# Two-layer graph kernel: block 0 of x turned by VectorE, and three reorderings

## Chip, cores and metric

The kernel runs on one core of a Trainium2 chip. The metric is the device time of one execution in microseconds (us), as a median over runs. The engines are named as in the profile: PE is TensorE (PEld its weight loads), DVE is VectorE, ACT is ScalarE, POOL is GpSimd, SP is SyncE, which here only issues DMAs. ACT and POOL issue DMAs too.

## The reference

x is 4096 x 512 (float32), adj is 4096 x 4096 (int32, 0 or 1, about 32 ones in a row). Two layers follow each other, each with a residual and a layer norm.

```python
# layer 0
keep = Ab & (cumsum(Ab, axis=1) <= 64)           # Ab = adj > 0: the first 64 neighbours
cnt = keep.sum(axis=1, keepdims=True)
nb_mean = (keep @ x) / maximum(cnt, 1)
xj = leaky_relu(nb_mean @ W_nb.T + b_nb)
xi = leaky_relu(x @ W_line.T + b_line)
x = layernorm(x + xi + where(cnt > 0, xj, 0))
# layer 1
Wh = x @ W + bW
e = leaky_relu((Wh @ a1 + b1)[:, None] + (Wh @ a2 + b2)[None, :], 0.2)
attention = softmax(where(adj > 0, e, -9e15), axis=1)
x = layernorm(x + attention @ Wh)
```

## The kernel before

The rows of x form 32 blocks of 128. All instructions of an engine run in the order in which the code emits them (`manual_schedule`); engines meet by semaphores only. So the order of the work is written out by hand, and what stands in front of a waiting instruction on its engine is fixed. A hardware DMA of SP or ACT takes one of eight semaphores in turn and waits until the last transfer with that semaphore has landed.

**Opening (layer 0).** The kernel forms y = x @ W_nb.T and the line term x @ W_line.T. A product on PE needs its left operand with the channels on the partitions, so the blocks of x and the weights must be turned. `turn_by_pe` (L310 and L153) does it in four steps: VectorE copies a 128 x 512 tile in another order, PE transposes four 128 x 128 squares of it into PSUM, and ScalarE copies the result to SBUF (L154). Both weight matrices go this way (`turn_w`, one row chunk of 128 at a time, `raw[name][c]`), and so does block 0 of x. The other blocks are turned by `turn_x` in one VectorE instruction (L325), a transpose of 32 x 32 squares; for it `load_turned_x` (L298) brings the block in four DMAs of 64 KB, 512 bytes a piece, so that each square's place is already right. Their landing places are the three tiles of `late`, used in turn. `load_w` (L351) sends the four chunks of a weight matrix to the given queues in turn. `spin` (L357) is a number of transposes of the identity that nobody reads; they fill PE's time while it waits for data.

`linear` (L372) is four matmuls of 128 x 128 by 128 x 512. For block 0 the product with W_nb is split: first its columns 0 to 383, which need only the chunks 0 to 2 of w_nb, then the turning of two chunks of w_line, then the last 128 columns.

`y_terms` splits y into a high part (ScalarE, L420) and a low part (VectorE, L421), both float32r. `line` adds the bias (VectorE, L405), `bend` is the leaky ReLU on ScalarE (L409), `own` stores the term to DRAM by POOL (L416).

**Blocks 2 to 25 (`seven`).** Pairs of blocks are multiplied by seven products instead of eight; `seven(g, ...)` writes out one pair's order, with the end of the pair before in between. PE's products are at L498. In each step g, VectorE adds `tt(bank_w, tg, x_g)` at L582; after it PE may go on adding into `x_g` (the product with `t3` in the next step). That addition waits for two ScalarE copies, L566 (`tg`) and L573 (`t0`).

Into the same steps, at four points `codes[0]` to `codes[3]`, the work on adj is woven. adj comes in chunks of 128 rows by 2048 columns (1 MB, `load_adj`, SP, L164) into two tiles in turn. `edge` (ScalarE, L175) makes flags from a chunk; `scan_sums` and `scan_codes` (VectorE, L193 to L206) count neighbours and make codes; `pack` (ScalarE, L223) turns the codes into bytes, which POOL writes to DRAM (L226). The order in step g, with q the number of the chunk:

```python
first = [lambda: edge(0), lambda: (load_adj(q + 2), edge(q + 1))]
steps = [
    first[g > 2],
    lambda: scan_sums(q),
    (lambda: pack(q - 1)) if g > 2 else first[1],
    lambda: scan_codes(q),
]
```

In g = 3, where q = 1, the flags of the third chunk (`edge(2)`) thus stand at `codes[0]` and the packing of the first chunk at `codes[2]`. In g = 1 the same points carry `fold_w`, sums over the third weight matrix (VectorE, L389).

**After that** come blocks 26 to 31 one by one, the product of the kept flags with y (PE, L750, from 214 to 678 us), layer 1's Wh, and the attention (PE, L1067, from 779 us on).

**Wh of layer 1 (`seven_wh`).** The first two pairs (`PLAIN`) are plain products, L1190; the others, g = 2 to 15, take seven products (PE, L887). In part 0 of a step, PE makes two products, ScalarE copies the first one to `m1` (L906), and VectorE adds `xv[:, 0] = m1 + yr[:, 1]`. For g = 2 that sum stands at L911, ahead of the turning of a later block (`turn_x1`, L833, of a tile that `load_turned` brings by DMA) and of `sums_x1` (L876, L877). For g > 2 it stands at L915, behind them. PE needs the sum for the first product of part 1.

Of the kernel before, what the change touches and what calls it, by code (L numbers as in the profile page):

```python
# [20 lines left out]
P = 128  # L21
SQ = 32
# [10 lines left out]
def two_layer_adj_gnn(  # L33
# [16 lines left out]
    nc = tc.nc  # L50
    N, C = x.shape
# [85 lines left out]
    with ExitStack() as l0:  # L137
# [22 lines left out]
        def load_adj(s):  # L160
            if s < NB * NCH:
                b, h = divmod(s, NCH)
                a = adj_p.tile([P, CH], I32, name="a")
                nc.sync.dma_start(a, adj_blk(b)[:, ts(h, CH)])  # L164
                loaded[s] = a
# [5 lines left out]
        def edge(s):  # L171
            if s < NB * NCH:
                b, h = divmod(s, NCH)
                edge_of[s] = halves_of(adj_p.tile([P, CH], BF16, name="edge"))
                nc.scalar.activation(  # L175
                    edge_of[s], loaded.pop(s).rearrange("p (t q) -> p q t", q=2),
                    AF.Sigmoid, bias=steep[:, 0:1], scale=STEEP,
                    accum_out=cnts[:, h, b : b + 1],
                )
# [39 lines left out]
        def pack(s):  # L219
            if 0 <= s < NB * NCH:  # L220
                b, h = divmod(s, NCH)
                code = adj_p.tile([P, CH // 2], BF16, name="code")
                nc.scalar.copy(  # L223
                    code.bitcast(U8).rearrange("p (t q) -> p q t", q=2), seen_of.pop(s)
                )
                nc.gpsimd.dma_start(code_d[b][:, ts(h, CH // 2)], code)  # L226
# [56 lines left out]
        with ExitStack() as la:  # L283
# [9 lines left out]
            def load_turned_x(i, queue=nc.gpsimd):  # L293

                if i < NB:
                    xrs[i] = late[i % 3].rearrange("p (j c) -> p j c", c=P)
                    for n in range(NC):
                        queue.dma_start(  # L298
                            xrs[i][ts(n, SQ)],
                            x_blk(i)[:, ts(n, P)].rearrange("(j a) c -> a j c", a=SQ),  # L300
                        )

            def load_own_x(i, queue):
                xbs[i] = work.tile([P, C], F32, name="xb", bufs=1)
                queue.dma_start(xbs[i], x_blk(i))

            def turn_by_pe(dst, src):

                t = work.tile([P, C], F32, name="t", bufs=4)
                nc.vector.tensor_copy(  # L310
                    t.rearrange("p (m n b) -> p m n b", m=NC, b=SQ),
                    src.rearrange("p (n m b) -> p m n b", m=NC, b=SQ),
                )
                transpose_to(dst, lambda m: t[:, ts(m, P)], NC)
# [4 lines left out]
            def turn_x(i, t=None):  # L319
                if i < NB:  # L320
                    xts[i] = xt_tile() if t is None else t
                    if i == 0:
                        turn_by_pe(xts[i], xbs[i])
                    else:
                        nc.vector.transpose(  # L325
                            xts[i].rearrange("p m (j a) -> p j m a", a=SQ),
                            xrs.pop(i).rearrange("p j (m b) -> p j m b", b=SQ),
                        )


            def early(name):
# [17 lines left out]
            def load_w(name, src, queues):  # L349
                for c in range(NC):  # L350
                    queues[c % len(queues)].dma_start(raw[name][c], src[ts(c, P), :])  # L351

            def spin(n):

                idle = ps_acc.tile([P, P], F32, name="acc")
                for _ in range(n):
                    nc.tensor.transpose(idle, ident, ident)  # L357

            def turn_w(name, idle=0, parts=range(NC)):

                if name not in w_t:
                    w_t[name] = wp.tile([P, NC, C], F32, name=f"wt_{name}")
                for c in parts:
                    if idle:
                        spin(idle)
                    turn_by_pe(w_t[name][:, :, ts(c, P)], raw[name][c])

            def linear(lhs_t, name, bank=None, part=slice(0, C)):

                pl = ps_acc.tile([P, C], F32, name="acc") if bank is None else bank  # L370
                for k in range(NC):
                    nc.tensor.matmul(  # L372
                        pl[:, part], lhs_t[:, k, :], w_t[name][:, k, part],
                        start=(k == 0 and part.start == 0),
                        stop=(k == NC - 1 and part.stop == C),
                        skip_group_check=part.stop - part.start < C,
                    )
                return pl

            def load_rows(queue):  # L380
# [37 lines left out]
            def y_terms(i, src):  # L418

                nc.scalar.copy(y_hi[i], src)  # L420
                return lambda: nc.vector.tensor_tensor(  # L421
                    y_lo[i], src, y_hi[i].bitcast(F32), ALU.subtract
                )

            load_own_x(0, nc.sync)
            load_w("nb", w_nb, (nc.scalar, nc.sync))
            load_turned_x(1, nc.sync)
            load_w("line", w_line, (nc.scalar, nc.sync))
            nc.sync.dma_start(bias_line, b_line.partition_broadcast(P))
            spin(15)  # L430


            turn_x(0)
            turn_w("nb", 2)

            for i in (2, 3):
                nc.vector.memset(late[i % 3][:, 0:1], 0.0)
                load_turned_x(i)
            pys[0] = linear(xts[0], "nb", part=slice(0, 3 * P))
            turn_w("line", 0, range(0, 2))  # L440
            linear(xts[0], "nb", pys[0], slice(3 * P, C))
            turn_w("line", 0, range(2, 4))
# [60 lines left out]
            turn_pair(1, 0)  # L503
            tt(t1, w12, w11, ALU.subtract)
            tt(t2, w22, t1, ALU.subtract)
            y_low = y_terms(0, pys[0])
            x_low[1] = xt_tile()
            turn_pair(1, 1)
            y_low()
            line(0)  # L510
            bend(0)
            pls[1] = linear(xts.pop(1), "line")
            wide.append(pls[1])
            x_top[0] = xt_tile()
            y_low = y_terms(1, pys[1])
            sums_x(1)
            own(0)
            y_low()
            load_adj(0)
            line(1)  # L520
            bend(1)
# [77 lines left out]
            for g in range(1, EDGE // 2):  # L599
                steps = idle  # L600
                q = done[0]
                if g == 1:
                    steps = [
                        lambda: (load_adj(1), fold_w(0)),
                        lambda: (fold_w(1), fold_w(2)),
                        idle[0],
                        lambda: (fold_w(3), fold_w(NC), fold_end()),
                    ]
                else:
                    first = [lambda: edge(0), lambda: (load_adj(q + 2), edge(q + 1))]  # L610
                    steps = [
                        first[g > 2],
                        lambda: scan_sums(q),
                        (lambda: pack(q - 1)) if g > 2 else first[1],
                        lambda: scan_codes(q),
                    ]
                    done[0] += 1
                seven(g, False, steps)
# [112 lines left out]
        for s in range(NB * NS):  # L731
            i, g = divmod(s, NS)
# [159 lines left out]
    def seven_wh(g, part, extra=lambda: None):  # L892

        p = g - 1
        new, old = g < NS // 2, p >= PLAIN
        yr, xv = yrs[g % 2], xvs[g % 2]
        yr_p, xv_p = yrs[p % 2], xvs[p % 2]
        t1, t2, t3, t4 = wsums  # L900
        m1 = bt[:, g, 2] if new else None
        if part == 0:
            if new:
                product_wh(yr[:, 0], x1ts[2 * g][:, 0:2], w11, start=True)
                product_wh(yr[:, 1], x1ts[2 * g + 1][:, 0:2], t3)
                nc.scalar.copy(m1, yr[:, 0])  # L906
            if old:
                product_wh(yr_p[:, 0], x1ts.pop(2 * p)[:, 2:4], w21)
                product_wh(xv_p[:, 1], sum_x(p, 1), t1)
            if g == PLAIN:  # L910
                nc.vector.tensor_tensor(xv[:, 0], m1, yr[:, 1], ALU.add)  # L911
            turn_x1(2 * g + 3)
            sums_x1(g + 1)
            if new and g > PLAIN:
                nc.vector.tensor_tensor(xv[:, 0], m1, yr[:, 1], ALU.add)  # L915
            if old:
                nc.scalar.copy(bt[:, p, 0:2], yr_p)
            extra()
        else:
            if old:  # L920
                product_wh(xv_p[:, 0], x1ts.pop(2 * p + 1)[:, 2:4], t4)
            if new:
                product_wh(xv[:, 0], sum_x(g, 2), t2)
                product_wh(yr[:, 1], sum_x(g, 4), w22)
            turn_x1(2 * g + 4)
            sums_x2(g + 1)
            if old:
                nc.scalar.copy(bt[:, p, 2:4], xv_p)
                later.append(p)
            if new:  # L930
                nc.scalar.copy(xv[:, 1], xv[:, 0])
            extra()
# [384 lines left out]
```

## Time and profile before

| | us |
|---|---|
| median of 3 runs | 1560.03 (1559.98 to 1561.58) |
| the profiled execution, its own time | 1561.81 |
| the profiled execution, its span | 1559.9 |
| PE busy | 1546.9 |
| VectorE busy | 1261.9 |
| ScalarE busy | 980.1 |

The page describes one profiled execution. Its span runs from the first to the last instruction; the time of that execution is 1.9 us more, and lies 1.8 us above the median of the other runs. A line of a timeline gives the start, the time taken, the engine, the line of the kernel, the operation, what it writes and reads, and in brackets how long the engine had been idle before it and what ended that. A float32 matmul is recorded as two passes, so x8 stands for four matmuls.

### The profile page before, as it was taken

What the parts mean: (1) busy time and instruction counts of PE and PEld (TensorE: products, weight loads), DVE (VectorE), ACT (ScalarE), POOL (GpSimd) and SP (SyncE); (2) the same over time, 40 slices, a digit from 0 to 9 for tenths busy, and PEclk for the clock granted to TensorE, in tenths of its full rate; (3) what the DMA queues carried; (4) which work ended last, traced back from release to release, by engine and by line L of the source; (5) the groups of instructions that cost most, each with busy time, mean ns of one, the idle gap of its engine ahead of it and who ended that gap; (6) DMA issues with size and microseconds to landing.
All of it is one profiled execution on the core that took longest, in us unless ns stands there. A gap on an engine that the chain in (4) does not pass through costs nothing.

```text
span 1559.9 us, 19141 instructions
## 1 busy us (share of the span) xinstructions
PE 1546.9 (99%) x6587; PEld 1242.7 (80%) x6587; DVE 1261.9 (81%) x2339; ACT 980.1 (63%) x1183; POOL 266.4 (17%) x424
## 2 busy tenths in 40 slices
PE   9999999999999999999999999999999999999998
PEld 5444468888888888868888888888888888888887
DVE  6888658999999999469888788887888878888864
ACT  2776558887888878427684576555775556755520
POOL 4554212222122122110001001110011110111101
PEclk9999999999999999999999999999999999999999
DMA  8866469988898988654122122221222211222102
GB/s 236 205 219 203 155 175 256 249 257 259 241 257 242 255 217 239 141 132 114 50 55 67 34 49 69 55 68 38 44 69 56 66 43 39 69 62 61 49 6 54
DMA packets 175425, 201.17 MB, mean 129 GB/s; under 512 B 102032, under 2 KB 135568, under 8 KB 167136
## 3 DMA queue, kind: packets, MB, share of 16 engines
q1 hardware_dynamic: 147472, 130.33, 30.4%
q0 software_dynamic: 26224, 67.64, 16.9%
q10 hardware_dynamic: 1632, 1.98, 0.4%
q8 instruction: 51, 0.84, 0.2%
q14 instruction: 46, 0.38, 0.1%
HBM read 141.03 MB, written 42.08 MB: 117 GB/s over the span
## 4 chain that ended last, share of the span: by engine, by line
PE 95%; DMA 2%; DVE 2%; issue 1%; ACT 0%; ACTq 0%; POOL 0%; POOLq 0%; DVEq 0%
PE acc L1067 35%; PE acc L750 30%; PE pt L1067 14%; PE acc L498 7%; PE acc L887 5%; PE acc L372 3%; DMA a<-in_adj_dram 1%; DMA w<-x_d 1%; PE pt L372 0%; PE pt L153 0%; PE acc L357 0%; DVE edge L389 0%; ACT edge L175 0%; DMA nat<-code_d 0%; DVE y_lo L421 0%
## 5 line engine op out<-in xcount | busy, mean ns | idle before, releaser
L1067 PE MATMUL acc<-bt,s 128*128 128x256 f32 x1504 | 335.7, 379 | 0.0
L750 PE MATMUL acc<-y_hi,kt 128*128 128x512 f32 x824 | 320.5, 389 | 0.0
L750 PE MATMUL acc<-y_lo,kt 128*128 128x512 f32 x824 | 320.5, 389 | 0.0
L1067 PEld LDWEIGHTS acc<-bt,s 128*128 128x128 f32 x1504 | 285.8, 190 | 38.9
L952 ACT ACTIVATE w<-nat,few 128x1024 f32<-128x1024 uint8 x128 | 137.0, 1136 | 237.8 <-DVE a L1027 237.8
L1067 PE MATMUL acc<-bt,a 128*128 128x256 f32 x1056 | 239.0, 379 | 0.0
L1067 PE MATMUL pt<-bt,a 128*128 128x256 f32 x992 | 224.5, 379 | 0.0
L1067 PEld LDWEIGHTS acc<-bt,a 128*128 128x128 f32 x1056 | 200.6, 190 | 27.3
L1067 PEld LDWEIGHTS pt<-bt,a 128*128 128x128 f32 x992 | 188.5, 190 | 25.6
L1027 DVE STREAM_TRANSPOSE a<-w 128x1024 f32<-128x1024 f32 x128 | 153.1, 1225 | 61.8 <-ACT w L1008 51.0
L277 ACT ACTIVATE kt<-ktb,few 128x1024 fp32r<-128x1024 uint8 x124 | 142.7, 1151 | 96.0 <-PE acc L750 76.7
L126 POOL TENSOR_TENSOR rs<-ve,few 128x1 f32<-128x1 f32 x64 | 44.8, 700 | 810.8 <-DVE ve L124 810.6
L750 PEld LDWEIGHTS acc<-y_hi,kt 128*128 128x128 f32 x824 | 154.7, 188 | 32.1
L750 PEld LDWEIGHTS acc<-y_lo,kt 128*128 128x128 f32 x824 | 154.6, 188 | 32.1
L945 ACT ACTIVATE w<-w,st_n 128x1024 f32<-128x1024 f32 x128 | 149.3, 1232 | 16.1 <-DVE m L962 16.1
L1008 ACT ACTIVATE w<-w,nm 128x1024 f32<-128x1024 f32 x128 | 145.5, 1138 | 11.1 <-DVE nm L999 11.1
L962 DVE CUSTOM_DVE_ANT_0 w<-e_n,w 128x1024 f32<-128x1024 f32 x128 | 149.5, 1221 | 1.3
L175 ACT ACTIVATE edge<-a,few 128x2048 bf16<-128x2048 int32 x64 | 136.2, 2128 | 9.5 <-DMA a<-in_adj_dram 5.3
L223 ACT CAST code<-left 128x2048 uint8<-128x2048 bf16 x64 | 121.1, 1892 | 0.0
L206 DVE TENSOR_TENSOR left<-edge,left 128x2048 bf16<-128x2048 bf16 x64 | 78.4, 1225 | 2.2
L298 POOL DMA_DIRECT2D c<-in_x_dram x120 | 66.1, 558 | 68.9 <-DVE xt L325 54.1
L194 DVE TENSOR_TENSOR_SCAN left<-few,ends,left 128x1024 bf16<-128x1024 f32 x32 | 75.2, 2351 | 1.1
(225 smaller groups left out, 2004.9 us busy)
## 6 DMA issues: line engine op xcount, KB each, us to landing
a<-in_adj_dram SPq DMA_DIRECT2D x64, 1024.0 KB, 6.3
code_d<-code POOLq DMA_DIRECT2D x64, 256.0 KB, 4.4
nat<-code_d SPq DMA_DIRECT2D x248, 64.0 KB, 2.2
w<-x_d SPq DMA_DIRECT2D x128, 64.0 KB, 2.1
own<-in_x_dram SPq DMA_DIRECT2D x31, 256.0 KB, 3.4
own<-own_d POOLq DMA_DIRECT2D x31, 256.0 KB, 5.0
x_d<-own POOLq DMA_DIRECT2D x31, 256.0 KB, 5.1
c<-in_x_dram POOLq DMA_DIRECT2D x120, 64.0 KB, 5.0
```

The lines of the kernel that those rows point to most:

```text
L175: nc.scalar.activation(edge_of[s], loaded.pop(s).rearrange("p (t q) -> p q t", q=2), AF.Sigmoid, bias=steep[:, 0:1], scale=STEEP, accum_ou ...
L206: nc.vector.tensor_tensor(left, e, left, ALU.mult)
L223: nc.scalar.copy(code.bitcast(U8).rearrange("p (t q) -> p q t", q=2), seen_of.pop(s))
L277: nc.scalar.activation(kts[s], bytes_.rearrange("p t (i r) -> p t r i", r=2), AF.Sigmoid, bias=steep[:, 1:2], scale=STEEP,)
L498: nc.tensor.matmul(bank, lhs[:, k, :], rhs[:, k, :], start=start and k == 0, stop=k == 1, skip_group_check=True,)
L750: nc.tensor.matmul(accs[i], kt[:, k // 2, k % 2, :], term[j], start=(j == 0 and term is y_hi), stop=(j == NB - 1 and term is y_lo),)
L945: nc.scalar.activation(dst, src, AF.Prelu, bias=bias, scale=scale, alpha=0.2)
L952: nc.scalar.activation(wts[b][:, i, :], nats[b, i // 2].bitcast(U8)[:, i % 2, :], AF.Relu, bias=far, scale=-FAR,)
L962: nc.vector.tensor_tensor_reduce(w_i, e2_n, w_i, 1.0, -3e38, ALU.subtract, ALU.max, m4s[b][:, i : i + 1])
L1008: nc.scalar.activation(w_i, w_i, AF.Exp, bias=nms[b][:, i : i + 1], accum_out=z4s[g][:, r, i : i + 1])
L1027: nc.vector.transpose(a[:, r].rearrange("p s (i a) -> p i s a", a=SQ), wts[2 * g + r][:, :, ts(k, 8 * SQ)].rearrange("p i (s x) -> p i s x ...
L1067: nc.tensor.matmul(banks[g][n], lhs[:, j, :], bt[:, 4 * k + j, rhs, :], start=(k == 0 and j == 0 and n == mate[0]), stop=(k == NP - 1 and ...
```

## The change

1. Block 0 of x is loaded in four DMAs like the others, ahead of everything else on SP, and turned by VectorE. The chunks 0 and 1 of w_nb are loaded by ACT and 2 and 3 by SP, instead of in alternation. On PE, 14 idle transposes stand at the start instead of 15. The chunks 0 to 2 of w_nb are turned, two idle transposes ahead of each, then block 0 on VectorE; the chunk 3 is turned behind the first matmul of block 0's product, without idle transposes.
2. The two y terms of blocks 0 and 1 are emitted together, ahead of the turning of block 3 and of block 0's line term. Before, they stood behind and between these.
3. In g = 3 of `seven`, the packing of the first chunk and the flags of the third change places. (In g = 2 and from g = 4 on, the order stays.)
4. In `seven_wh`, the sum for g = 3 stands ahead of the turning, as for g = 2.

```diff
             def turn_x(i, t=None):
                 if i < NB:
                     xts[i] = xt_tile() if t is None else t
-                    if i == 0:
-                        turn_by_pe(xts[i], xbs[i])
-                    else:
-                        nc.vector.transpose(...)
+                    nc.vector.transpose(
+                        xts[i].rearrange("p m (j a) -> p j m a", a=SQ),
+                        xrs.pop(i).rearrange("p j (m b) -> p j m b", b=SQ),
+                    )
...
-            def linear(lhs_t, name, bank=None, part=slice(0, C)):
+            def linear(lhs_t, name, bank=None, part=slice(0, C), behind_first=lambda: None):
...
+                    if k == 0:
+                        behind_first()
...
-            load_own_x(0, nc.sync)
-            load_w("nb", w_nb, (nc.scalar, nc.sync))
+            load_turned_x(0, nc.sync)
+            load_w("nb", w_nb, (nc.scalar, nc.scalar, nc.sync, nc.sync))
             load_turned_x(1, nc.sync)
             load_w("line", w_line, (nc.scalar, nc.sync))
             nc.sync.dma_start(bias_line, b_line.partition_broadcast(P))
-            spin(15)
-            turn_x(0)
-            turn_w("nb", 2)
+            spin(14)
+            turn_w("nb", 2, range(3))
+            turn_x(0)
             for i in (2, 3):
                 nc.vector.memset(late[i % 3][:, 0:1], 0.0)
                 load_turned_x(i)
-            pys[0] = linear(xts[0], "nb", part=slice(0, 3 * P))
+            pys[0] = linear(
+                xts[0], "nb", part=slice(0, 3 * P), behind_first=lambda: turn_w("nb", 0, range(3, 4))
+            )
...
-            y_low = y_terms(0, pys[0])
+            for i in range(2):
+                y_terms(i, pys[i])()
             x_low[1] = xt_tile()
             turn_pair(1, 1)
-            y_low()
             line(0)
             bend(0)
             pls[1] = linear(xts.pop(1), "line")
             wide.append(pls[1])
             x_top[0] = xt_tile()
-            y_low = y_terms(1, pys[1])
             sums_x(1)
             own(0)
-            y_low()
             load_adj(0)
...
-                    first = [lambda: edge(0), lambda: (load_adj(q + 2), edge(q + 1))]
+                    flags = lambda: (load_adj(q + 2), edge(q + 1))
+                    codes = (lambda: pack(q - 1)) if g > 2 else (lambda: edge(0))
                     steps = [
-                        first[g > 2],
+                        flags if g > 3 else codes,
                         lambda: scan_sums(q),
-                        (lambda: pack(q - 1)) if g > 2 else first[1],
+                        codes if g > 3 else flags,
                         lambda: scan_codes(q),
                     ]
...
-            if g == PLAIN:
+            if g < PLAIN + 2:
                 nc.vector.tensor_tensor(xv[:, 0], m1, yr[:, 1], ALU.add)
             turn_x1(2 * g + 3)
             sums_x1(g + 1)
-            if new and g > PLAIN:
+            if new and g >= PLAIN + 2:
                 nc.vector.tensor_tensor(xv[:, 0], m1, yr[:, 1], ALU.add)
```

More of the change, by code (lines that the diff above doesn't have):

```diff
@@ L321, in turn_x @@
                     xts[i] = xt_tile() if t is None else t
-                    if i == 0:
-                        turn_by_pe(xts[i], xbs[i])
-                    else:
[L325 to L328, printed above, removed]
+                    nc.vector.transpose(
+                        xts[i].rearrange("p m (j a) -> p j m a", a=SQ),
+                        xrs.pop(i).rearrange("p j (m b) -> p j m b", b=SQ),
+                    )
             def early(name):
```

## The prediction

> **What bounds the kernel now.** I read the page first, for the busy shares and the chain that ended last.
>
> ```profile
> PE 1546.9 (99%) x6587; PEld 1242.7 (80%) x6587; DVE 1261.9 (81%) x2339; ACT 980.1 (63%) x1183; POOL 266.4 (17%) x424
> ...
> PE 95%; DMA 2%; DVE 2%; issue 1%; ACT 0%; ACTq 0%; POOL 0%; POOLq 0%; DVEq 0%
> ```
>
> TensorE (PE) is busy 1546.9 of 1559.9 us. The change removes no work from it but four transposes and three of the idle transposes that fill the opening. So it can gain only where PE stands still or does filler. The view of waits, for PE alone, has all standstills but the end:
>
> ```profile
> PE acc L498 <- DVE acc L582: 2.1, 3, 1.2
> PE acc L357 <- POOL ident masks.py:199: 1.4, 1, 1.4
> PE acc L887 <- DVE acc L911: 0.9, 1, 0.9
> PE acc L887 <- DVE acc L915: 0.8, 1, 0.8
> PE acc L498 <- DVE y_lo L421: 0.4, 1, 0.4
> ```
>
> Without the 1.4 us before the first instruction, 4.2 us are to be had. 0.2% of 1560 us, about what a measurement of this kernel can tell from no change, is 3.1 us. PE's timeline places the waits (start, duration, then the idle time before):
>
> ```profile
> 8.97 2.85 PE L372 MATMUL acc<-wt_nb,xt 128*128 128x384 f32 x8
> ...
> 25.16 1.98 PE L498 MATMUL acc<-wt_nb,xt 128*128 128x512 f32 x4 [0.41 <-DVE y_lo L421]
> ...
> 34.33 1.98 PE L498 MATMUL acc<-wt_line,xt 128*128 128x512 f32 x4 [0.28 <-DVE acc L582]
> ...
> 60.94 1.98 PE L498 MATMUL acc<-wt_line,lo 128*128 128x512 f32 x4 [1.23 <-DVE acc L582]
> ```
>
> From 8.97 to 24.6 and from 60.94 to 678 us PE never waits, so a time won or lost at the front stays to the end, if the others keep up. Of L582's three waits the one not shown is 0.59 us at 47.44. A stall costs about 0.16 us more than its idle time: the product before it could have been followed after 59.55 (eight passes of 0.43 from 56.12), not after its modelled end.
>
> **What the Trainium skill says.** "VectorE: DVE Perf Modes", The three transpose paths: VectorE turns only 32x32 blocks, so the rest of the turning must lie in the load. The trace agrees: one STREAM_TRANSPOSE of 128x512 f32, 0.70 us, after four loads of 64 KB. "DMA: Bandwidth & Descriptors", Queues, rings and completion order: SP and ACT have a ring each on the same 16 engines, which serve the rings in turn. The trace agrees: from 3 to 4 us 93 packets of SP's queue and 100 of ACT's. "TensorE: Matmul & The Clock Gate", Part 1: PE starts throttled, speeds up after about 3.4 us of work, and falls back after as long an idle stretch. The trace agrees on the start (0.23 us for one idle transpose at first, 0.11 after 6.4 us); it has no idle gap that long, so the fall is not shown.
>
> **The change, part by part.** Below, nb0 to nb3 and line0 to line3 are the four row chunks of w_nb and w_line; x0 and x1 are the blocks of x.
>
> *Block 0 turned by VectorE (opening).* Removed: a VectorE copy (0.43), four PE transposes, a ScalarE copy (0.59). Added: one STREAM_TRANSPOSE (0.70) and three more DMA issues on SP (0.3 to 0.4 each), as x0 now comes in four pieces. The first products need nb0 to nb2; now nb0, nb1 lie on ACT's queue and nb2, nb3 on SP's behind x0's pieces. DMA is full from 3 us on (share 1.03 to 1.10 in the windows), so order decides. In the packet records a 2048-byte packet takes 84 ns and a 512-byte one 27 to 30, so a 256 KB chunk is 128 x 84 / 16 = 0.67 us of all engines and an x piece 0.24. Now the loads landed at 4.55 (two chunks done, 1.34 of work), 5.8 (four, 2.69) and 7.5 (six and one piece, 4.27): work plus 3.2. After: before nb2 come x0 (0.96), nb0, nb1, line0, line2 (2.69), then itself: 4.32 + 3.2 = 7.5; 6.85 if line2 still stands behind it. I take 7.4. nb2's path is then copy 0.38, transposes 0.44, ScalarE copy 0.59 and three hand-overs of 0.1: first product at 9.1 instead of 8.97. x0 lands earlier, and its transpose ends inside this path. nb3's four transposes, which PE did before 8.97, now stand behind the first product: 0.44 and 0.1 for the hand-over. **Sum: 0.7 us lost; I take 0.6.** Bounds: -0.5 (nb2 at 6.3, small packets going ahead), +1.5 (nb2 at 8.3). Queued behind: nb3 and then x1's pieces and line1, line3 on SP (issues that wait for earlier landings; line1 now for line2's). Total bytes are the same and line1 landed at 10.1 for a need at 12.1, so that is hidden by 2 us. POOL's loads of x2 and x3 start after the two memsets, about 1 us later; x2 is first needed at 24.6, and was turned at 14.1: hidden. VectorE's later work is hidden by its 3.7 us of idle time before 21.36.
>
> *Two y terms sooner.* y_lo of blocks 0 and 1 (0.57, 0.60) leave the stretch from 22.0 to 25.0 and go into VectorE's idle time before 21.36; ScalarE's y_hi of block 1 follows, 6 us sooner (ScalarE idle 7.7 us). PE's wait at 25.16 goes. But the next wait, at 34.33, is for VectorE's L582, and VectorE runs without a gap from 21.36 to 34.27. It gets 1.17 us free, yet line(1) must wait for PE's end of block 1's line product at 24.76; it starts at 24.85 instead of 25.02. So only **0.2 us** of 0.57 is kept, and the waits at 34.33 and 47.44 remain, the former larger. Bounds: 0.1 and 0.3.
>
> *Flags of the third chunk later.* ScalarE's timeline:
>
> ```profile
> 51.65 0.57 ACT L556 COPY acc<-acc 128x512 f32<-128x512 f32 x1 [3.22 <-DVE y_lo L421]
> 55.78 2.15 ACT L175 ACTIVATE edge<-a,few 128x2048 bf16<-128x2048 int32 x1 [3.56 <-DMA a<-in_adj_dram]
> ...
> 59.58 0.58 ACT L573 ACTIVATE t<-acc 128x512 f32<-128x512 f32 x1
> 60.06 1.89 ACT L223 CAST code<-left 128x2048 uint8<-128x2048 bf16 x1
> ```
>
> ScalarE waits 3.56 us for the chunk with four operations queued behind it; L582 waits for the last (L573), PE for L582. Now pack (1.89, its input ready at 50.4) takes that place: 52.2 to 54.1, the four follow to about 56.4, and L582 comes at 56.9, bound by VectorE's own scan, against PE's need at 59.5. The flags start at 56.4, after the landing at 55.8, and end at 58.6, when ScalarE's next copies are due and VectorE is still busy to 60.6. **Gain 1.39 us** (1.23 and 0.16). SP: the fourth chunk's load waits on flags of the second, done at 47.4 as before; the fifth is issued at about 58.7 instead of 58.0. POOL: the code write (0.56) comes 8 us sooner, ahead of four loads of x issued at 55.6. What is late next: the fourth chunk landed at 59.5 and its flags, still first in g = 4, come up at about 62; 256 KB more in a full DMA costs it 0.7. Cover 1.8 us; if it is gone, up to 1.4 comes back.
>
> *One sum of wh sooner (g = 3).*
>
> ```profile
> 699.68 0.71 DVE L833 STREAM_TRANSPOSE a<-w 128x512 f32<-128x512 f32 x1 [0.59 <-DMA w<-x_d]
> 700.43 0.43 DVE L876 TENSOR_TENSOR bt<-a 128x256 f32<-128x256 f32 x1
> 700.89 0.42 DVE L877 TENSOR_TENSOR a<-a 128x256 f32<-128x256 f32 x1
> 701.23 0.42 DVE L915 TENSOR_TENSOR acc<-bt,acc 128x256 f32<-128x256 f32 x1
> ```
>
> The sum's ScalarE input is ready at 698.76. It now goes at 699.1, in the 0.59 us that VectorE waits for a load, so transpose and differences keep their times. PE, that started the product at 701.71, can at 700.8: **0.9 us** (0.5 to 0.93: VectorE is dense to 713, and the sum of g = 5 is then just in time).
>
> **Sum** against the profiled execution (span 1559.9, its own time 1561.8, 1.8 above the median): 0.6 - 0.2 - 1.4 - 0.9 = -1.9 us. I apply the difference to the median 1560.03: **1558.1 us**.
>
> **Rivals.** (A) As summed, 1558.1; 0.50. (B) The opening pays too: the removed copies had held nb0 to nb2 up (nb2 landed at 5.8, its PE transposes started only at 7.67), so if nb2 lands by 6.3 the opening gains 0.6 and with 2.5 the sum is -3.1 or more: 1556.8. Against it: four ACT chunks stand in turn with x0. 0.24. (C) A stall comes back: the fourth chunk's flags hold ScalarE in g = 4, or wh's later sums hold PE: 1559.4. For it: DMA full from 52 to 65 us. 0.20. (D) Slower: PE runs dry in the opening. After two chunks and its fillers it has nothing from about 6.4; if nb2 lands at 9.4, the gains are eaten; from about 10.2 (line1's landing now) the gap is over the skill's 3.4 us, and PE's clock falls back: an estimate of 3.4 us at half speed, 1.7 us. Then 3.3 + 1.7 - 2.5: 1562.5, past 0.2% from nb2 at 10.9. Against it: nb2 waits only for nb0's landing. 0.06.
>
> **How the numbers follow.** B alone is faster by over 0.2%: 0.24. A and C are within: 0.70. D: 0.06. The range runs from just under B's value, 1556.6, to just short of no change, 1559.9; A's own, from its bounds, is 1557.0 to 1559.2.
>
> **What would show it.** Right: the first 128x384 product at about 9.1; no PE wait at 60 us nor on L916 near 701; the one after g = 1 (L581) 0.3 larger; ScalarE's pack at 52 us. Wrong: a PE wait on L581 near 71, a first product after 10, an idle transposes' pace of 0.23 us again after 7 us, or one before 8.5, which is B.

## The result, and the profile after

The kernel after takes 1562.75 us (median of 22 runs, 1560.35 to 1564.61), the kernel before 1560.03 (22 runs, 1559.05 to 1562.14). The ratio is 1.0018, 95% interval [1.0011, 1.0024]: 2.8 us slower, [1.7, 3.7], where 1.9 us faster was forecast; the median lies outside the predicted range, 1556.6 to 1559.9. The profiled execution of after has a span of 1562.8 us and an own time of 1564.61. That is 1.9 us above its median, as before's was 1.8 above its own, but it is also the longest of the 22, so what is read off this profile is after at its worst.

The page of after, busy shares and the chain that ended last:

```profile
PE 1548.9 (99%) x6580; PEld 1243.4 (80%) x6580; DVE 1262.6 (81%) x2339; ACT 981.2 (63%) x1182; POOL 268.4 (17%) x424
...
PE 97%; DVE 1%; DMA 1%; ACT 0%; issue 0%; SPq 0%; POOLq 0%; DVEq 0%; ACTq 0%
```

TensorE has seven instructions fewer (four transposes, three idle ones), and yet 2.0 us more busy time. It worked at a lower pace somewhere. PE's waits (us in total, times, longest):

```profile
PE pt L153 <- DVE t L310: 2.2, 2, 2.0
PE acc L354 <- POOL ident masks.py:199: 1.4, 1, 1.4
PE acc L888 <- DVE acc L912: 0.9, 1, 0.9
PE acc L499 <- DVE acc L581: 0.9, 2, 0.6
PE acc L369 <- ACT wt_nb L154: 0.7, 1, 0.7
PE acc L888 <- DVE acc L916: 0.2, 1, 0.2
PE acc L499 <- ACT acc L596: 0.2, 1, 0.2
```

Against before, the 1.23 us at 61 us, in step g = 3 (L582 then, L581 now), the 0.41 us on y_lo and the 0.76 us on a sum of wh are gone or small. New are 1.96 us at the turning of w_nb (the copy L310) and 0.68 us at the first product (ScalarE's copy of the turned chunk, L154). PE's timeline (start, duration; idle time before, with its releaser):

```profile
7.04 0.38 PE L354 MATMUL acc<-ident 128*128 128x128 f32 x2
9.37 0.78 PE L153 MATMUL pt<-ident,t 128*128 128x128 f32 x4 [1.96 <-DVE t L310]
10.82 1.65 PE L369 MATMUL acc<-wt_nb,xt 128*128 128x384 f32 x2 [0.68 <-ACT wt_nb L154]
12.27 1.06 PE L153 MATMUL pt<-ident,t 128*128 128x128 f32 x4
13.12 3.80 PE L369 MATMUL acc<-wt_nb,xt 128*128 128x384 f32 x6
16.76 1.04 PE L153 MATMUL pt<-ident,t 128*128 128x128 f32 x8
```

The first product starts at 10.82 (before: 8.97), the transposes of line0 and line1 behind it at 16.76 (before: 11.65). So 5.11 us are lost by 17 us. The view of windows, in which the number in front of the DMA share is the granted clock of TensorE, says how:

```profile
9.00:10.00 1.00, 0.63 (x4) 0.42 (x4) 0.97 (x5) 0.00 (x0) 0.00 (x0) 0.86 1.26 210
10.00:16.00 6.00, 5.32 (x12) 3.25 (x12) 3.18 (x8) 1.17 (x2) 5.81 (x10) 0.50 0.83 213
16.00:17.00 1.00, 1.00 (x5) 0.49 (x5) 0.00 (x0) 0.00 (x0) 1.00 (x3) 0.73 0.99 336
```

PE ran at half speed from 9.72 to 16.55 (the ends are from the clock's own records); before, all these windows stood at 1.00. The loss of 5.11 us can be split, with the full-clock run e4 as the yardstick:

- the first product is later by 10.82 - 8.97 = 1.85 us;
- nb3's transposes now lie inside the product: where the clock is full (e4 below) it takes 3.13 us from its start to line0's transposes, before it took 2.68: 0.45 us;
- at half clock the same stretch takes 5.94 us: 5.94 - 3.13 = 2.81 us.

Later parts give back some of it. The shift of equal products, after less before, is +4.88 at the wait at 39.21, +3.51 at the y product at 64.45 and +2.37 at 705.04; it ends at +2.9, the difference of the spans. All these shifts compare one execution with one other. The seven profiles with the old opening (before, e1, e5, e6, e7, e10, e11) start the transposes of line0 between 10.93 and 13.78 us, at 11.70 on average, so before's 11.65 is a fair measure of it.

### The profile page after: what moved, and what is told of

It is laid out like the page before. It is cut to its first block, busy times and chain, and to the rows that moved or that the text cites. A ratio compares the mean times of both kernels' runs of the same rounds, so it can differ in the third digit from the quotient of the medians.

```text
span 1562.8 us, 19137 instructions
## 1 busy us (share of the span) xinstructions
PE 1548.9 (99%) x6580; PEld 1243.4 (80%) x6580; DVE 1262.6 (81%) x2339; ACT 981.2 (63%) x1182; POOL 268.4 (17%) x424
## 3 DMA queue, kind: packets, MB, share of 16 engines
q10 hardware_dynamic: 1632, 1.98, 0.5%
## 4 chain that ended last, share of the span: by engine, by line
PE 97%; DVE 1%; DMA 1%; ACT 0%; issue 0%; SPq 0%; POOLq 0%; DVEq 0%; ACTq 0%
PE acc L1068 35%; PE acc L751 30%; PE pt L1068 14%; PE acc L499 8%; PE acc L888 5%; PE acc L369 3%; PE acc L1191 1%; DMA a<-in_L_gnn_W_nb_dram 1%; PE pt L369 0%; DVE edge L388 0%; PE pt L153 0%; DVE left L194 0%; ACT edge L175 0%; DMA nat<-code_d 0%; ACT L175 0%
```

## Experiments

Theory T: the opening loses the time, through a first product that comes late and a clock that falls in the gap ahead of it; the other three parts pay about what was forecast. Rivals: lateness alone, the clock being a bystander; a later part costs what it should have won; and, once sizes came in, that the forecast gains belonged to one execution. Differences below are the ratio's excess over 1, times 1560 us. Each ratio is taken against the kernel before at the same time on the same chip; the median of before there was 1559.75 to 1561.26 us. So two changed kernels measured at different times are compared through their ratios.

### e1_rest_only and e2_open_only: where the loss lies

e1 is after with the opening of before, e2 is before with the new opening alone. The edit of e1 (e2 is its complement: these lines as in after, all others as in before):

```diff
-            load_turned_x(0, nc.sync)
-            load_w("nb", w_nb, (nc.scalar, nc.scalar, nc.sync, nc.sync))
+            load_own_x(0, nc.sync)
+            load_w("nb", w_nb, (nc.scalar, nc.sync))
...
-            turn_w("nb", 2, range(3))
             turn_x(0)     # i == 0: turn_by_pe again
+            turn_w("nb", 2)
...
```

> The changed kernel with the opening of before (block 0 turned by PE, w_nb in alternation on the two queues); the y terms, the flags and the sum of wh stay changed. Theory (the whole loss lies in the opening): the three reorderings bring 0.2 + 1.4 + 0.6 = 2.2 us, so about 1557.8 us, first 128x384 product at 9.0 us. Rival (a part of the loss lies in the reorderings, through later waits of POOL or SP): 1559 or more.

> The kernel before with the new opening alone. Theory: first product at about 10.8 us and the opening 5.1 us later at its end, of which 2.8 are PE's half clock: about 1565 us, with a wide spread between executions[...]. Rival (the opening is late by its data alone, 2.3 us): 1562.3. Rival (the old stalls at 34, 47 and 61 us swallow a part): 1563.

Measured: e1 ratio 0.9988 [0.9982, 0.9995], 1.9 us faster. e2 1.0022 [1.0014, 1.0029], 3.4 us slower [2.2, 4.5]; its profile shows a gap of 1.85 us, a first product at 10.60 and the clock at half from 8.80 to 15.63. The loss lies in the opening, and the three later parts together gain; that they cost what they should have won is ruled out.

Two expectations missed. The first product of e1, with the old opening, was expected at 9.0 and came at 11.10:

```profile
11.10 2.85 PE L372 MATMUL acc<-wt_nb,xt 128*128 128x384 f32 x8
```

In that execution block 0 was copied at 5.26 (before: 4.38), and the clock's record shows full speed only from 10.0 us (before: 6.5). So the old opening has late executions too.

e2 was expected 5.1 us over before, with a wide spread, and is 3.4. The 5.1 had been read off a profile with the clock at half, and the clock doesn't fall in every execution. For each execution the clock granted over the whole span is on record, to three places. An execution with 0.999 lost less than 2.4 us to a lower clock. In the profiles the end of the kernel alone takes 1.2 to 2.5 us, and a fall of 3.41 us in the opening takes 1.7 more; so with 0.999 there was no fall in the opening. One with 0.997 or less lost over 3.9 us, so there was one; 0.998 leaves it open. In e2 the five executions with 0.999 have a median of 1563.35, 2.1 us above before, and the five with 0.997 or less one of 1566.14, 4.9 above. The same opening thus costs about 2 us where it is only late, and 2.8 more where the clock falls. In after, 11 of 22 executions have 0.997, 10 have 0.998 and one has 0.999.

### e3_fill and e9_half_fill: lateness or clock

e3 fills PE's gaps with idle transposes and moves nothing else; e9 fills half of the first gap.

```diff
-            turn_w("nb", 2, range(3))
+            turn_w("nb", 2, range(2))
+            turn_w("nb", 20, range(2, 3))     # e9: 10 in place of 20
             turn_x(0)
...
+            spin(5)                           # e3 alone
             pys[0] = linear(xts[0], "nb", ...
```

> The changed kernel with 20 idle transposes instead of 2 ahead of the third chunk of w_nb and 5 ahead of the first product, so that PE is not idle while it waits; transfers unchanged. Theory (2.8 us of the loss are the clock): PE clock full from 6 us on, third chunk lands at 8.8 as before, first product at about 10.8, the end of the first part 2.8 us sooner: about 1560.0 us. Rival (the products behind 10.8 are slow because they wait for data): no change, 1562.7.

> The kernel after with 10 idle transposes instead of 2 ahead of the third chunk of w_nb, and none ahead of the first product: by 0.11 us each (20 took 2.35 us) they leave about 1.0 us of the 1.96 us gap, and the 0.68 us gap ahead of the first product stays. If an idle stretch has to fill about 2 us before the clock falls, the clock holds and the time is that of the kernel with the whole gap filled, 1.0 to 1.3 us over before's 1560 less the gains of the other parts: about 1560. If what counts is idle time in the fixed 3.4 us stretch, however it is cut up, 1.0 + 0.68 us of idleness is near what the kernel after had and the clock falls in some or all executions: about 1562.5. If lateness alone made the loss, also 1562.5, with a full clock in the profile.

e3: 0.9999 [0.9991, 1.0008], so 3.0 us better than after (the two intervals lie 0.5 us apart). Its timeline:

```profile
9.33 0.63 PE L153 MATMUL pt<-ident,t 128*128 128x128 f32 x4
9.79 0.71 PE L354 MATMUL acc<-ident 128*128 128x128 f32 x5
10.63 0.91 PE L369 MATMUL acc<-wt_nb,xt 128*128 128x384 f32 x2
11.38 0.60 PE L153 MATMUL pt<-ident,t 128*128 128x128 f32 x4
11.82 2.10 PE L369 MATMUL acc<-wt_nb,xt 128*128 128x384 f32 x6
13.75 1.04 PE L153 MATMUL pt<-ident,t 128*128 128x128 f32 x8
```

The chunk's transposes and the first product come as late as in after (9.33 and 10.63 for 9.37 and 10.82), but six products take 2.10 us instead of 3.80. "Lateness alone" is refuted: work that computes nothing gives 3.0 us back, against 2.81 us read off the timeline. What e3 still lacks to e1 is 1.7 us, against 2.3 of lateness in the split above.

e9: 1.0003 [0.9995, 1.0011], 2.3 us better than after. Its timeline:

```profile
9.41 0.63 PE L153 MATMUL pt<-ident,t 128*128 128x128 f32 x4 [1.10 <-DVE t L310]
10.72 1.37 PE L369 MATMUL acc<-wt_nb,xt 128*128 128x384 f32 x2 [0.68 <-DVE t L310]
11.88 1.06 PE L153 MATMUL pt<-ident,t 128*128 128x128 f32 x4
12.73 2.96 PE L369 MATMUL acc<-wt_nb,xt 128*128 128x384 f32 x6
```

In this execution the clock fell at 11.04 for 3.41 us, half as long as in after, and no single gap was over 1.10 us. So a fall doesn't need one long gap: 1.10 + 0.68 us of idleness within one stretch of 3.41 us (7.63 to 11.04) went ahead of this one. The time lies near the case "the clock holds", the profile shows a fall. The granted clocks agree with both: the profiled execution is the longest of 13, ten have 0.999 (median 1561.0), and the three with 0.998 are the longest (1562.26 to 1563.26). In most executions half the filling was enough.

### e4_nb_act and e8_x_pool: can nb2 come sooner

SP issues nb2 late in after. SP's timeline of after, and its waits up to 20 us:

```profile
0.75 1.82 SPq L298 DMA_DIRECT2D c<-in_x_dram  x4
4.76 0.83 SPq L348 DMA_DIRECT2D a<-in_L_gnn_W_nb_dram  x2
```

```profile
SPq L348 <- DMA a<-in_L_gnn_W_nb_dram: 2.5, 2, 2.2
```

SP has x0's four pieces out by 2.6 and then stands until 4.76, because nb2's issue waits for nb0's landing (4.74). nb2 lands at 8.77, 4.0 us later, as nb0 took from its issue. There are two candidates for the lateness: this wait, and the place behind x0's pieces in SP's queue. e4 gives nb2 to ACT's queue; e8 leaves w_nb alternating and gives x0 to POOL's queue.

```diff
 e4:
-            load_w("nb", w_nb, (nc.scalar, nc.scalar, nc.sync, nc.sync))
+            load_w("nb", w_nb, (nc.scalar, nc.scalar, nc.scalar, nc.sync))
 e8:
-            load_turned_x(0, nc.sync)
-            load_w("nb", w_nb, (nc.scalar, nc.scalar, nc.sync, nc.sync))
+            load_turned_x(0)
+            load_w("nb", w_nb, (nc.scalar, nc.sync))
```

> The changed kernel with the third chunk of w_nb on ACT's queue ahead of w_line, so that it does not wait on SP for the first chunk's landing nor stand behind block 0's pieces. Theory (the place in the queue made it late, and the gap made the clock fall): it lands at about 7.3 as the fifth 256 KB of both queues, PE's gap is 0.6 us, clock full, first product at 9.4: about 1558.7 us. Rival (the pieces of 512 bytes slow every packet beside them, so the chunk is late in any queue): lands after 8.3, 1561 or more.

> The changed kernel with block 0's four pieces on POOL's queue and w_nb in alternation on ACT and SP as before. Theory (the pieces ahead on SP made w_nb late): the first three chunks land by 5.8 us as before or sooner, the pieces at about 6.5 to 7, the first product starts at about 8.0, clock full: 2.5 us less than before on the same chip. Rival (pieces of 512 bytes delay everything beside them in any queue, or POOL's issue is too slow): first product after 9, less than 1.5 us gained.

e4: 0.9989 [0.9983, 0.9996], 1.7 us faster than before. Its timeline:

```profile
7.57 0.60 PE L153 MATMUL pt<-ident,t 128*128 128x128 f32 x4
8.84 0.91 PE L369 MATMUL acc<-wt_nb,xt 128*128 128x384 f32 x2 [0.68 <-ACT wt_nb L154]
9.59 0.60 PE L153 MATMUL pt<-ident,t 128*128 128x128 f32 x4
10.03 2.10 PE L369 MATMUL acc<-wt_nb,xt 128*128 128x384 f32 x6
11.97 1.04 PE L153 MATMUL pt<-ident,t 128*128 128x128 f32 x8
```

nb2 is copied at 6.59 instead of 8.80, the gap ahead of its transposes is gone, the 0.68 us gap alone leaves the clock full, and line0's transposes start at 11.97. So one word in a list of queues turns the change's loss into a gain. It stands level with e1 (1.9), so block 0's turning by VectorE is worth nothing measurable even where its loads come right. e4 and e1 are both a little faster than before and than after; these runs don't tell which is the better.

The packet records tell the two candidates apart. In after, SP's queue moves x0's packets of 512 bytes until 6.63 us, in turn with ACT's of 2048 bytes, and nb2's first packet starts at 7.14. In e4 it is nb3 that stands behind x0 on SP. It is issued at 3.84, 0.9 us sooner than nb2 in after, and yet its first packet starts only at 6.64, when x0's last ones go out. So by these two executions an earlier issue could have brought nb2 forward by 0.5 us at most; the rest goes with its place behind the small packets. 256 KB in packets of 512 bytes held SP's queue until 6.6 us, as long as 768 KB in packets of 2048 did in before (until about 6.5).

e8 missed: 1.0028 [1.0018, 1.0038], 4.4 us slower. nb2 was copied at 6.11, but x0's pieces, issued by POOL from 1.5 to 3.9, landed only by 10.6, and the first product, at 11.42, had waited 3.97 us for block 0's turning, with the clock at half from 12.75 to 16.16. A late load, PE idle, then the clock at half: the path is the same as in after, with another load.

### e5_only_flags, e6_only_sum, e7_only_y: the other parts singly

Each is before with one part of the change:

```diff
 e5 (flags):
-                        first[g > 2],
+                        flags if g > 3 else codes,
...
-                        (lambda: pack(q - 1)) if g > 2 else first[1],
+                        codes if g > 3 else flags,
 e6 (sum):
-            if g == PLAIN:
+            if g < PLAIN + 2:
...
-            if new and g > PLAIN:
+            if new and g >= PLAIN + 2:
 e7 (y):
-            y_low = y_terms(0, pys[0])
+            for i in range(2):
+                y_terms(i, pys[i])()
... (the old places of the y terms are emptied)
```

> The kernel before with the exchange of pack and flags in g = 3 alone. Theory: the PE wait of 1.2 us near 61 us goes and nothing takes its place: 1.4 us less than before on the same chip. Rival (the fourth chunk's flags in g = 4 stall ScalarE in its turn): a PE wait near 71 to 73 us and less than 0.7 us gained.

> The kernel before with the sum of wh for g = 3 ahead of the turning, alone. Theory: the PE wait of 0.8 us at 701.7 goes (0.9 us in starts), and a part comes back at the sum of g = 5, because VectorE's turning waits for a load and is not earlier: a wait of 0.2 to 0.3 us on that sum, 0.6 us net. Rival (as predicted, 0.9 us net): no PE wait on that sum.

> The kernel before with the y terms of blocks 0 and 1 together, alone. Theory: the PE wait at 25 us (0.41) goes, about 0.2 us is kept, the waits at 34 and 47 us stay at 0.3 and 0.6, since VectorE must wait for block 1's line product: 0.2 us less, not to be told from nothing by the times. Rival (VectorE is freed by 1.2 us): the waits at 34 and 47 us go, 1 us or more gained.

Measured: e5 0.9997 [0.9989, 1.0006], 0.5 us faster; e6 0.9994 [0.9986, 1.0002], 0.9; e7 1.0000 [0.9992, 1.0008]. No interval leaves out either the forecast or zero, so the times of single parts settle nothing here; their sum, 1.4, goes with e1's 1.9. In the profiles each part does what was expected of it: in e5 no stall at 61 us and none near 71; in e6 the stall on the sum of g = 3 gone and 0.41 us on the sum of g = 5; in e7 the 0.41 us on y_lo gone, the waits at 33 and 47 us at 0.28 and 0.60. The profiles tell more, for an unexpected reason: in e6 and e7, which leave the flags where they were, the stall of 1.23 us at 61 us is absent.

### e10_y_and_sum and e11_before_again: how firm is the stall at 61 us

e10 is before with the parts of e6 and e7 together; e11 is the kernel before, unedited, in a new execution.

> The kernel before with two of the four parts alone: the y terms sooner and the wh sum sooner; opening and flags as before. If the flags' stall of 1.23 us at 61 us stands in every execution and putting the flags later takes 1.4 us out, then this kernel lacks that gain: 1.9 - 1.4 = 0.5 us below before, 1559.5. If the stall comes and goes with the landing of the third chunk of adj, as the two runs whose profiles lacked it suggest, it lacks little: 1.0 to 1.9 us below before, 1558.1 to 1559.

> The kernel before, unchanged, in another execution: does the stall on the y product at 61 us (1.23 us in its first profile, 1.31 us with the new opening, absent in two others that left the flags in place) stand? If the flags' order alone makes it, 1.2 to 1.3 us again. If the landing of the third chunk of adj makes it, anything from 0 to 1.3 us, and the wait of the third chunk's flags for their load moves with it (3.56 us in the first profile, 2.26 and 1.98 us where the stall was absent).

e10: 0.9997 [0.9988, 1.0005], 0.5 us faster, nearer to the case "the flags lack 1.4" and with an interval that holds both. e11, one execution: 1560.5 us, with a stall of 0.88 us. ScalarE's timeline of e11 has the wait for the third chunk of adj, PE's the stall that follows:

```profile
55.05 2.16 ACT L175 ACTIVATE edge<-a,few 128x2048 bf16<-128x2048 int32 x1 [3.20 <-DMA a<-in_adj_dram]
```

```profile
60.22 1.98 PE L498 MATMUL acc<-wt_line,lo 128*128 128x512 f32 x4 [0.88 <-DVE acc L582]
```

The same of e6, ScalarE's timeline and PE's waits up to 80 us:

```profile
53.85 2.16 ACT L175 ACTIVATE edge<-a,few 128x2048 bf16<-128x2048 int32 x1 [2.26 <-DMA a<-in_adj_dram]
```

```profile
PE acc L500 <- DVE acc L584: 0.9, 2, 0.6
```

In e6 L584 (the L582 of before) is waited for twice, at 34 and 47 us, and not at 61. Over the six profiles that keep the flags' old order:

| kernel | ScalarE waits for the chunk, us | PE stalls at 60 to 66 us, us | difference |
|---|---|---|---|
| e2 | 3.65 | 1.31 | 2.34 |
| before | 3.56 | 1.23 | 2.33 |
| e10 | 3.32 | 0.99 | 2.33 |
| e11 | 3.20 | 0.88 | 2.32 |
| e6 | 2.26 | 0 | |
| e7 | 1.98 | 0 | |

In all six the old order hides 2.33 us of the wait; what is over passes to PE one for one. The mean stall is 4.41 / 6 = 0.74 us, not 1.23. What moves is the landing of the chunk. Ahead of it, from about 41 us on in before, some 25 packets of 4096 bytes on POOL's queue take up to 7 or 8 us each, and the DMA engines move next to nothing (0 to 16 GB/s from 42 to 48 us). The last slow one ended at 49.66 in before, 48.87 in e11, 48.66 in e10, 47.68 in e6 and 47.43 in e7: nearly the order of the stalls. Just before, at 37 to 39 us in before, SP's queue carries 1040 packets of 4 bytes (the store of `wa_d`). Whether they are why the packets behind them are slow was not tried. The stall on wh's sum moves as well: with the sum of g = 3 in its old place 1.35 (e2), 0.76 (before), 0.50 (e7), 0.34 (e11) and 0 us (e5).

## Why the prediction was wrong, point by point

- **Opening, "0.7 us lost; I take 0.6": the step that failed.** It measured 5.11 us in the profile, and 4.7 by the runs (after's +2.8 less e1's -1.9). It was mis-sized in two terms, the landing of nb2 and the clock.
  - *Landing, "work plus 3.2", nb2 at 7.4.* nb2 landed at 8.77, beyond the bound of 8.3. That it would stand behind x0's pieces was foreseen, but the formula was fitted to loads in large packets: it takes the work as if DMA moved it at the same rate. It did not. Up to 9 us DMA moved 213 GB/s for 251 before, and the packets of 2048 bytes on ACT's queue took 116, 147 and 133 ns (medians in the three microseconds from 4 to 7) beside those of 512 bytes, for the 84 ns of the working. So x0 left SP's queue only at 6.63. The wait of nb2's issue for nb0's landing, which rival D's text named and took for a comfort, cost at most 0.5 us of the 1.37 by which nb2 was late; the rest goes with the slower queue. From nb2's landing to the first product it took 2.05 us, not 1.7; some 0.15 of it is the clock already (from the chunk's transposes to the product 1.45 us, in e3 1.30), the rest lies in the hand-overs between the engines. e4 shows that the late landing is the cause: nb2 on another queue, and the loss is gone.
  - *The clock, put at nothing in the likeliest case.* It cost 2.81 us in the profiled execution, and less or nothing in others (e2 above). The Trainium skill, "TensorE: Matmul & The Clock Gate", Part 1, led the prediction to ask for a gap of 3.4 us, which rival D put at nb2 landing from 10.2 on. Here a gap of 1.96 us was enough, and in e9 one of 1.10 with one of 0.68: the measurement decides. e3 shows the price.
- **Rival D** (6 in 100) was the right mechanism, PE dry ahead of nb2 and then slow. Its 1562.5 us meets the result by luck, with sizes that were off: the gap shorter than it asked for, the half clock 2.81 us instead of 1.7, the lateness 2.3 instead of 3.3. It should have had more than 6 in 100, since the gap's length was unproven on both sides.
- **nb3's transposes, 0.54**: 0.45 measured. Right.
- **Two y terms, 0.2**: from 16.76 to 39.21 the shift falls from 5.11 to 4.88, so 0.23. Right. PE's wait of 0.41 us on y_lo went; 0.22 us on ScalarE's L596, at 31.80, stands in its place. That the wait behind g = 1 would grow by 0.3 was wrong: it stayed at 0.28 (and the next one at 0.59).
- **Flags, 1.39**: from 52.33 to 64.45 the shift falls from 4.89 to 3.51, so 1.38, and ScalarE's pack stands ahead of the four operations as foreseen. Right for these two executions; but the term was read off an execution with a high stall, and the mean of six is 0.74.
- **Sum of wh, 0.9**: the product comes 1.02 us sooner (the shift falls from 3.39 at 703.31 to 2.37 at 705.04), then about half of it is lost again. The prediction had said "the sum of g = 5 is then just in time"; it was not. VectorE's and PE's timelines of after:

```profile
702.40 0.42 DVE L912 TENSOR_TENSOR acc<-bt,acc 128x256 f32<-128x256 f32 x1
703.39 0.71 DVE L834 STREAM_TRANSPOSE a<-w 128x512 f32<-128x512 f32 x1 [0.56 <-DMA w<-x_d]
```

```profile
716.67 1.13 PE L888 MATMUL acc<-s,bt 128*128 128x256 f32 x4 [0.24 <-DVE acc L916]
```

  The sum went out early at 702.40, yet VectorE still waits 0.56 us for a load behind it, so all that follows on VectorE is no sooner; PE, that had come 1.0 us nearer, meets the sum of g = 5 with a stall of 0.24 us. The other profiles with the sum sooner have 0.4 (e3, e6), 0.16 (e9) or none (e1, e4, e8, e10).
- **Rivals B and C.** B's landing of nb2 by 6.3 did not occur; e4 comes near it (copied at 6.59) and gains nothing over before's opening, so B's mechanism was worth less than it claimed. C's stall on the fourth chunk did not come: the flags at 67 us go without a wait. Its second half, wh's later sums, is the 0.24 us above.

The forecast for the three later parts, 2.5 us, stands against 1.9 [0.8, 2.8] in e1. Of the error of 4.7 us, 4.1 lie in the opening.

## What to carry to other kernels

When a load changes its queue, look at what stands ahead of it there and in what packets: here small packets, served in turn with large ones, held a queue as long as three times their bytes in large packets. Then see when it can be issued at all. A count of bytes ahead of it gives only a lower bound. Where PE is the bound and has to stand still for a load early on, look at how much idle time falls together within a few microseconds, and price the slow stretch behind it: fillers that compute nothing were worth about 3 us here. A stall read off one execution may be a transfer's luck; take a second execution before you book it as a gain.

## What the runs showed of the hardware

- Where the clock fell in the opening, its records are multiples of 3.413 us long: half for 6.83 us in after and e2, for 3.41 in e8 and e9. The stretch ahead of the fall held 1.96 us of idle time in after, 1.8 in e2, 1.10 + 0.68 in e9 and 2.1 in e8; 0.68 us in e4 did not make it fall. No threshold follows: e8 had 1.9 us idle in the stretch from 5.92 to 9.34 as well, and kept its clock in the next one.
- Where these stretches begin differs between executions of like openings: full clock from 4.4, 4.7, 4.8, 5.1, 6.5, 7.2 and 10.0 us in e6, e10, e11, e7, before, e5 and e1. That the clock falls in some executions and not in others is shown by the granted clocks (e2, e9); that the place of these stretches decides it is argued, not shown. After's times spread over 4.3 us, e3's, with the gaps filled, over 1.2.
- A queue of 512-byte packets beside one of 2048-byte packets is slow for its bytes: 256 KB took SP's queue from 1.82 to 6.63 us in after, while ACT's packets of 2048 bytes took 116 to 147 ns instead of 84.
- Four loads of 64 KB issued on POOL's queue at 1.5 to 3.9 us, while the queues of SP and ACT were full, landed only by 10.6 us (e8); on SP's queue in after, issued from 0.75 on, they landed by 7.5.
